# A table of offsets for the parts of a scheduled two-mixer kernel, and a larger constant for VectorE's dependent instructions

## The chip, the cores and the metric

The kernel runs on one core of a Trainium2 chip. The metric is the device time of one execution in microseconds; lower is better. Three runs of the kernel before the change give the median that is quoted, and one execution was taken by the hardware profiler.

## The reference, cut to what matters

The input x is an image batch of 4 x 256 x 64 x 64, that is 16,384 tokens of 256 channels, all in float32. Two layers follow each other; the second is a mixer and a mixture of experts.

```
# layer 0: Mamba, a selective scan over the 4,096 tokens of each image
tokens = tokens @ w_in.T
z = sigmoid(silu(tokens @ w_gate.T + b_gate))
t = layernorm(tokens)
xm, zm = split(t @ in_w.T)               # 512 + 512 channels
xm = silu(conv4(xm))                     # four taps along the tokens
dt, B, C = split(xm @ xproj_w.T)         # 16 states
h = exp(dt*A) * h + dt*x*B               # per channel and state, step by step
y = sum_n(h*C) + D*xm;  y = y * silu(zm)
x = tokens + (y @ out_w.T) * z @ w_out.T + x
# layer 1: Mamba-2 (SSD), 8 heads of 64, 64 states
xn = rmsnorm(ln(t));  z, xBC, dt = split(xn @ W_in.T);  xBC = silu(conv4(xBC))
state = state*exp(dt*A) + dt*x (x) B;  y = state.C + D*x
t = t + ln(t) + rmsnorm(y*silu(z)) @ W_out.T
# and 8 experts, top 1, capacity 2,560 tokens each, hidden 1,024
t = t + expert(ln(t)) * probability
```

## The kernel before, in words

There are three phases, one after the other: `mixers`, `experts` and `turn`. The change touches only the first.

**The mixers' work.** The tokens are cut into 64 chunks of 256, sixteen to an image. For each chunk the code records these groups of work:

- `front0`: loads the chunk (xin), makes the centred projection and the gate, the layer norm, the in-projection by m_in_w and the four-tap convolution (taps_m).
- `mid0`: stores the gates to DRAM (gx_d, z_d), makes B, C and dt (x_proj, dt_w), and stores bc_d, dt_d and u_d to DRAM. From there they come back in another layout: 32 channels times 4 states on the 128 partitions.
- `scan`: sixteen steps u = 4j + f. Each has a decay `da` (ScalarE, exp), `ub` = u4 times B (VectorE, into a PSUM tile with one buffer), for later chunks an addition of the carried state e0 to ub's first column, the scan h (VectorE, `tensor_tensor_scan`, 1,024 columns), `hlast` (ScalarE), `p` = h times C (GpSimd) and eight small products that sum p over the states into `py` (TensorE). h has three buffers, p two, da three, dt4 and u4 two, bc4 five.
- `tail0`: loads xtail and z, multiplies the gated tile g by m_out_w, and makes x1.
- `front1`: layer 1's norms (stats, logs, scale, shift), the projections by W_in, dt and the convolution (taps_x, from a copy in DRAM).
- `ssd`: layer 1's mixer in two halves s = 0 and 1 of 128 tokens: cum, decay and cdec (ScalarE and TensorE), gm, xdt and the products by decay and cdec (VectorE), the outputs and the new state.
- `back1`: out-projection, routing, and a scatter of each row to its expert's place.

Work of two chunks lies side by side: in the loop, chunk i's `front0` to `front1` are recorded beside `ssd` and `back1` of chunk i-2.

**What sets the order.** None of it is issued as it is recorded. The class `Plan` notes each instruction with an engine, a weight and its dependencies, and a list scheduler, `order()`, walks a clock of its own. When an engine is free on that clock, it takes, of the instructions whose inputs are ready and whose buffers have room, the one with the smallest key (slot, sequence number). The resulting order is the order of each engine's queue on the chip; on the chip each engine goes through its queue in that order and waits where an input is late. So the keys decide only between instructions that are ready at once, and there is no timed start. `BEHIND` is the time on that clock from the end of an instruction to a dependent one on the same engine, `SIGNAL` the same to another engine. GpSimd's p is marked `ride`: it is ordered behind the VectorE instruction before a scan, so that it runs beside the scan.

**The slots.** Sixteen slots make a chunk (`NST`). A part of the code begins with `k_.at(n)`, which sets the slot to 16i + n plus an offset found by the part's number in the chunk, `nth`, counting the calls of `at`:

```
def at(self, n):
    self.nth += 1
    r.slot(self.i * NST, n + SHIFT.get(self.nth, 0.0))
```

Counted through the code, the numbers are these. 0 to 12: front0 (0 is the load of xin, 3 and 4 the two halves of the in-projection, 6, 8, 10, 12 the convolutions). 13 and 14: the activations' call. 15 to 22: mid0 (15 is the store of gx_d and z_d, 16 x_proj, 22 the product u and its store). 23 to 26: the four bc4 loads. Then for each j from 27, 46, 65 and 84: the dt4 load, the u4 load, e0, and for each f four parts: da, ub with the scan, hlast with p, py. 103: the loads of xtail and z; 104: m_out and z; 105: x1 and stats; 106 to 121: the rest of front1 (120 is the last load of taps). 122 and 123: the second activations' call. 124 to 134: ssd (126 and 130 are cum of the two halves, 127 and 131 decay and cdec, 128 and 132 gm, xdt and their products, 129 and 133 the outputs). 135 to 141: back1 (138 and 140 are parts of the routing).

The slots that matter below are TAIL = 18 (m_out), SSD = 29, BACK = 37, FRONT0 = -25 and MID0 = -16. Before the change the table SHIFT is empty, so that every part has its plain slot. The weights on the scheduler's clock are formulas, for instance n/960 us plus 0.06 for a VectorE instruction of n columns.

**Line numbers.** Instructions of the mixers are issued by `Plan.issue`, so that the profile gives all of them line 373; they are told apart by the names of their tiles. PSUM tiles go by a (two buffers), b (one) and c (two).

Of the kernel before, what the change touches and what calls it, by code (L numbers as in the profile page):

```python
# [43 lines left out]
TAIL, SSD, BACK = 18, 29, 37  # L44
AHEAD = 4

SHIFT = {}
TOK = 4
ROW = TOK + C

# [86 lines left out]
class Plan:  # L137
# [4 lines left out]


    SIGNAL = {"DVE": 0.13, "ACT": 0.19, "PE": 0.21, "POOL": 0.12}
    BEHIND = {"DVE": 0.13, "ACT": 0.14, "PE": 0.0, "POOL": 0.13}
    LANES = 8
    SPARE = {}
    PATIENCE = 4.0
# [126 lines left out]
    def order(self):  # L275
# [34 lines left out]
        while done < len(self.ops):  # L310
# [6 lines left out]
            for e in engines:  # L317
# [40 lines left out]
                for u in op.users:  # L358
                    u.missing -= 1
                    late = op.end + (0.06 if op.lag else (self.BEHIND if u.engine == e else self.SIGNAL)[e])  # L360
                    u.ready = max(u.ready, late)
# [22 lines left out]
def tile_conv_attn_hybrid(ctx: ExitStack, tc: tile.TileContext, a: dict, out: bass.AP, cap: int, st: int):  # L384
# [45 lines left out]
    def mixers(es):  # L430
# [289 lines left out]
        class Chunk:  # L720
# [3 lines left out]
# [5 lines that stand above are left out]
# [842 lines left out]
```

## Time and profile before

| what | value |
|---|---|
| median of three runs | 6,706.08 us (6,697.39 to 6,709.94) |
| profiled execution | 6,706.9 us, span 6,704.9 us |
| mean granted TensorE clock | 0.957 |
| PE (TensorE) busy | 6,188.0 us, 92% |
| DVE (VectorE) busy | 5,552.4 us, 83% |
| ACT (ScalarE) busy | 4,879.5 us, 73% |
| POOL (GpSimd) busy | 3,295.2 us, 49% |
| first and last scan start | 80.9 us, 5,508.6 us |
| one scan, mean | 2,285 ns, 1,024 times |
| one p on GpSimd, mean | 2,355 ns, 1,024 times |
| one ub, mean | 1,250 ns, 1,024 times |

The shares are averages over the three phases, which have different limits; the mixers are read from stretches inside them. PE is the matmuls, PEld the loads of weights, which overlap them. A row of the groups gives line, engine, operation, output <- inputs, shape and count, then busy us and the mean of one in ns, then the idle time of the engine just before these instructions and what ended it. In the timeline the columns are start, length (both us), engine, line, operation and tiles, and in brackets the idle time before with what ended it.

### The profile page before, as it was taken

To read this page: it belongs to the slowest core of one execution; us is meant where nothing else is said; L and a number is where in the kernel's file an instruction comes from. 1 tells how busy PE (TensorE), PEld (TensorE's weight loads), DVE (VectorE), ACT (ScalarE), POOL (GpSimd) and SP (SyncE) were. 2 spreads that over 40 slices of the span, in tenths; PEclk is the share of its full clock that TensorE was granted. 3 is DMA by queue.
4 is the path that set the end of the run, shared out by engine and by line. 5 is a ranking of instruction groups with operands and counts; after the bars stand their busy time and mean duration, and the time that the engine had idled before them with its cause. 6 is when DMAs were issued, how large, how long until landed. Compare 5 with 4: busy or idle time off the path is not lost. (4 is left out here: it accounts for less than half of the span.)

```text
span 6704.9 us, 111610 instructions
## 1 busy us (share of the span) xinstructions
PE 6188.0 (92%) x37578; PEld 4282.6 (64%) x37578; DVE 5552.4 (83%) x7685; ACT 4879.5 (73%) x11999; POOL 3295.2 (49%) x2622
## 2 busy tenths in 40 slices
PE   7899999999999999999999999999999977999997
PEld 5566666666666666666666666666666646888886
DVE  5999999999999999999999999999999983434443
ACT  5888888888888888888888888888888863333333
POOL 4655555555555555555555555555555552333331
PEclk8999999999999999999999999999999988999998
DMA  6854445455555545455545555555555434555556
GB/s 188 234 149 150 150 147 151 146 151 152 152 153 152 149 145 151 146 150 150 152 148 150 153 153 153 153 153 152 151 153 152 149 102 143 199 199 195 200 197 260
DMA packets 924401, 1078.46 MB, mean 161 GB/s; under 512 B 93537, under 2 KB 895077, under 8 KB 912435
## 3 DMA queue, kind: packets, MB, share of 16 engines
q1 hardware_dynamic: 890002, 842.27, 42.2%
q0 software_dynamic: 29472, 212.28, 8.7%
q10 hardware_dynamic: 4352, 16.78, 0.6%
q8 instruction: 296, 4.85, 0.3%
q14 instruction: 279, 2.28, 0.1%
HBM read 787.00 MB, written 276.76 MB: 159 GB/s over the span
## 5 line engine op out<-in xcount | busy, mean ns | idle before, releaser
L373 POOL TENSOR_TENSOR p<-h,bc 128x1024 f32<-128x1024 f32 x1024 | 2411.3, 2355 | 2008.0 <-DVE ub L373 507.2
L373 DVE TENSOR_TENSOR_SCAN h<-da,ub 128x1024 f32<-128x1024 f32 x1024 | 2339.5, 2285 | 78.1 <-ACT da L373 5.8
L373 ACT ACTIVATE da<-dt,w_m_Alog 128x255 f32<-128x255 f32 x4096 | 1842.6, 503 | 0.0
L373 DVE TENSOR_TENSOR ub<-u,bc 128x1024 f32<-128x1024 f32 x1024 | 1279.7, 1250 | 13.3 <-DMA u<-u_d 5.9
L373 PE MATMUL py<-p,sum 128*32 128x256 f32 x8192 | 662.4, 396 | 183.4 <-POOL p L373 176.8
L373 PE MATMUL b<-t,w_W_in 128*128 128x256 f32 x2304 | 579.6, 392 | 25.6 <-ACT bcs L373 4.9
L373 PEld LDWEIGHTS b<-t,w_W_in 128*128 128x128 f32 x2304 | 418.7, 190 | 189.9 <-ACT raw L373 76.2
L373 PE MATMUL a<-t,w_m_in_w 128*128 128x256 f32 x2048 | 511.3, 393 | 3.1 <-DVE t L373 2.8
L1411 PE MATMUL ph<-xt,w 128*128 128x256 f32 (+1 forms) x2304 | 496.1, 368 | 12.2 <-ACT hid L1413 11.9
L373 PEld LDWEIGHTS py<-p,sum 128*32 128x32 f32 x8192 | 168.9, 108 | 508.0 <-POOL p L373 259.2
L373 PE MATMUL a<-raw,taps_m 128*128 128x256 f32 x2048 | 480.6, 382 | 4.8 <-ACT pre L373 4.8
L1422 PE MATMUL po<-w,hid 128*128 128x256 f32 x2160 | 478.0, 379 | 0.0
L373 PEld LDWEIGHTS a<-t,w_m_in_w 128*128 128x128 f32 x2048 | 371.3, 191 | 145.1 <-issue 73.3
L373 PEld LDWEIGHTS a<-raw,taps_m 128*128 128x128 f32 x2048 | 377.4, 189 | 130.1 <-ACT e L373 39.0
L1411 PEld LDWEIGHTS ph<-xt,w 128*128 128x128 f32 x2304 | 412.3, 190 | 69.5 <-ACT hid L1413 17.9
L1422 PEld LDWEIGHTS po<-w,hid 128*128 128x128 f32 x2160 | 409.7, 190 | 55.3
L373 ACT COPY hlast<-h 128x4 f32<-128x4 f32 x1024 | 202.9, 198 | 278.7 <-DVE h L373 266.1
L1385 DVE CAST number<-rows 128x2 uint32<-128x2 f32 x72 | 12.3, 170 | 450.1 <-DMA tok_d<-fixed,number 437.7
L1383 ACT ACTIVATE tn<-rows 128x256 f32<-128x256 f32 x135 | 77.4, 596 | 401.0 <-DMA rows<-buf_d,row_at 400.3
L1434 POOL DMA_INDIRECT tok_d<-fixed,number x135 | 138.5, 1026 | 402.6 <-DVE fixed L1432 265.0
L373 PE MATMUL c<-cum,after 128*128 128x512 f32 x512 | 321.1, 713 | 14.5 <-ACT dend L373 13.7
L373 ACT ACT_TABLE_LOAD x256 | 328.4, 1283 | 4.7
(237 smaller groups left out, 11312.0 us busy)
## 6 DMA issues: line engine op xcount, KB each, us to landing
dt<-dt_d SPq DMA_DIRECT2D x1024, 128.0 KB, 2.5
u<-u_d SPq DMA_DIRECT2D x1024, 128.0 KB, 2.3
raw<-raw_d SPq DMA_DIRECT2D x1024, 128.0 KB, 3.3
gx_d<-pre SPq DMA_DIRECT2D x64, 1024.0 KB, 4.5
bc<-bc_d SPq DMA_DIRECT2D x1024, 64.0 KB, 2.5
gx<-gx_d SPq DMA_DIRECT2D x256, 256.0 KB, 3.1
raw_d<-raw SPq DMA_DIRECT2D x64, 518.0 KB
dt_d<-mid SPq DMA_DIRECT2D x64, 512.0 KB, 3.2
```

Of the source, the lines that this page charges most:

```text
L373: op.issued = f(*map(placed, args), **{k: placed(v) for k, v in kw.items()})
L1383: act(tn[:, j], rows[:, j, TOK:], AF.Identity, scale=rows[:, j, 1:2], bias=rows[:, j, 2:3])
L1385: nc.vector.tensor_copy(number, rows[:, :, 3])
L1411: mm(ph, w1[:, k, f * P : (f + 1) * P], xt[:, k], start=k == 0, stop=k == KC - 1)
L1422: mm(po[:, j], hid[:, f, j * P : (j + 1) * P], w2[:, f], start=f == 0, stop=f == KF - 1)
L1434: nc.gpsimd.indirect_dma_start(out=tok_d, out_offset=bass.IndirectOffsetOnAxis(ap=number[:, j : j + 1], axis=0), in_=fixed[:, j], in_offse ...
```

## The change

Two edits. The table SHIFT, empty before, gets an offset in slots for 88 of the 142 parts, the same for each of the 64 chunks. And the scheduler's clock counts 0.17 us instead of 0.13 us from a VectorE instruction to a dependent one on VectorE. No recorded instruction, tile, buffer count or dependency differs; what differs is the order that `order()` gives to the engines' queues, and with it which instruction GpSimd's p is put behind.

```diff
-SHIFT = {}
+SHIFT = {
+    0: 3.3, 2: -0.2, 3: 1.0, 4: -0.7, 6: 0.9, 15: -2.7, 22: 0.4, 26: 5.5, 29: 0.9, 36: 0.1, 40: -0.6, 42: 0.4,
+    44: -0.1, 45: -6.6, 46: -0.1, 47: -0.1, 48: -1.1, 49: -0.4, 50: 0.2, 51: -0.1, 52: -0.1, 53: 0.9, 54: -0.1,
+    55: -0.1, 56: -0.1, 57: -0.1, 58: -0.1, 59: -0.1, 60: -0.1, 61: -1.6, 62: -0.1, 63: -0.1, 64: -0.1, 65: 0.9,
+    66: -0.1, 67: -0.1, 68: -0.1, 69: -0.1, 70: -0.1, 71: -0.4, 72: -0.1, 73: -0.1, 74: -0.1, 75: 1.2, 76: -0.1,
+    77: -0.1, 78: -0.1, 79: -0.1, 80: -2.6, 81: -0.1, 82: -0.1, 83: 3.0, 84: -0.1, 85: 1.4, 86: -0.1, 87: -0.1,
+    88: -1.9, 89: -0.1, 90: -0.1, 91: -0.1, 92: -0.1, 93: -1.1, 94: -1.7, 95: -0.5, 96: -0.1, 98: -0.1, 99: -0.1,
+    100: -0.1, 101: 0.1, 102: -0.1, 103: -7.4, 104: -2.5, 105: -0.1, 106: 0.9, 107: -0.1, 108: -0.1, 109: -0.1,
+    110: -0.1, 111: -0.1, 117: -0.1, 120: 3.4, 128: 0.9, 130: -1.4, 131: -0.6, 132: -0.1, 134: 0.3, 138: 2.0,
+    140: 0.5,
+}
...
-    BEHIND = {"DVE": 0.13, "ACT": 0.14, "PE": 0.0, "POOL": 0.13}
+    BEHIND = {"DVE": .17, "ACT": 0.14, "PE": 0.0, "POOL": 0.13}
```

## The prediction

> **What bounds the kernel now.** I read the page's table of 40 slices first: VectorE (DVE) and TensorE (PE) show a 9 in nearly every slice up to 5,500 us and the two part company only after it. So the mixers, 0 to 5,570 us, are the stage that the change can touch; the experts and the turn after it, 1,135 us, are built without the offsets. Then the busy table by stretch, whose columns are PE, PEld, DVE, ACT and POOL busy, clock and DMA:
>
> ```profile
> 1000.00:2000.00 1000.00, 937.23 (x5879) 615.91 (x5879) 926.72 (x1235) 816.13 (x2030) 521.17 (x399) 0.96 0.50 150
> 2000.00:3000.00 1000.00, 937.58 (x5951) 613.71 (x5952) 929.46 (x1226) 829.19 (x2055) 529.71 (x402) 0.96 0.51 149
> 3000.00:4000.00 1000.00, 936.12 (x5966) 612.82 (x5964) 938.04 (x1261) 830.26 (x2072) 534.20 (x414) 0.97 0.51 151
> 4000.00:5000.00 1000.00, 940.40 (x5983) 618.41 (x5981) 936.68 (x1251) 828.99 (x2068) 533.29 (x405) 0.97 0.51 152
> ```
>
> In these 4,000 us VectorE is busy 3,730.9 and TensorE 3,751.3. The groups of instructions give 750 scans, sixteen to a chunk, hence 46.9 chunks of 85.3 us. Per chunk VectorE sits idle 269.1/46.9 = **5.7 us** and TensorE 248.7/46.9 = 5.3 us. Neither is free of waits, neither has much to give: one order of work holds both. Third, VectorE's waits in the same 4,000 us (who <- for whom, us in total, times, longest):
>
> ```profile
> DVE cdec L373 <- ACT cdec L373: 62.9, 41, 3.4
> DVE stats L373 <- PE b L373: 60.5, 47, 3.9
> DVE xdt L373 <- PE c L373: 28.0, 89, 0.9
> DVE row L373 <- PE c L373: 23.2, 19, 1.3
> DVE gm L373 <- PE c L373: 14.3, 47, 0.8
> ```
>
> With the small ones this is 196.6 us, 4.2 per chunk; the other 1.5 are short gaps between VectorE's own dependent instructions. One more loss hides inside busy time:
>
> ```profile
> L373 DVE TENSOR_TENSOR decay<-decay,gm 128x1024 f32<-128x1024 f32 x93 | 178.2, 1916 | 0.0
> L373 DVE TENSOR_TENSOR decay<-decay,gm x93: 1215/1219/2833, 1017.1 to 4943.8; 128x1024 f32<-128x1024 f32 x93
> ```
>
> The mean, 1,916 ns, is far over the median of 1,219: 178.2 - 93 x 1.219 = 64.8 us, 1.4 per chunk. At most 4.2 + 1.4 + 1.5 = 7.1 us per chunk, 64 times = 454 us, could ever be won on VectorE.
>
> **What the Trainium skill says.** "SBUF — State Buffer", section "Who interferes with whom": a VectorE instruction with two SBUF inputs contends with a GpSimd instruction that reads SBUF, and the second to start blocks. The trace agrees: the decay product of 2.58 us at 4076.24 falls where GpSimd multiplies p; undisturbed ones take 1.22. "VectorE: DVE Perf Modes", section "The DRAIN you can't avoid": a semaphore between chained VectorE instructions costs nothing extra. The trace differs: in the rows near 3040 an instruction that uses its forerunner's result starts 0.13 us (ub after scan), 0.12 (e0 addition after ub) and 0.22 (scan after the addition) later than an independent one would. "Perfetto Trace Analysis", section "Tensor Engine Instruction (MATMUL, LD_WEIGHTS)": VectorE, ScalarE and GpSimd are strict FIFO. It agrees: when cdec waits 1.79 us below, the e0 addition and the scan behind it wait too.
>
> **The change part by part.** It adds and removes no instruction or byte; each item below is a move. One slot is 85.3/16 = 5.3 us, and an offset only decides between parts that are ready at once.
>
> *The constant for VectorE, 0.13 to 0.17.* The three measured spacings average 0.16, so the new number is about right. It adds at most 3 x 0.04 x 16 = 1.9 us per chunk to the order's own clock, no time on chip. It may lead the order to put a filler into some of the 1.5 us of gaps: bounds -0.5 to +0.2 us per chunk, taken **-0.15**.
>
> *Out projection two and a half slots earlier (104), second half of the SSD earlier (130: -1.4, 131: -0.6), its first half later (128: +0.9).* This is the place where the waits lie, so I read the order of time around one chunk's end:
>
> ```profile
> 4085.61 2.08 PE L373 MATMUL c<-cum,after 128*128 128x512 f32 x2
> 4087.61 1.99 PE L373 MATMUL a<-pre,w_m_xproj_w 128*64 128x256 f32 x8
> 4089.53 1.12 PE L373 MATMUL c<-cum,after 128*128 128x512 f32 x2
> 4090.59 1.08 PE L373 MATMUL c<-cum,ones 128*64 128x512 f32 x4
> 4091.60 3.72 PE L373 MATMUL b<-g,w_m_out_w 128*128 128x256 f32 x16
> ...
> 4084.33 0.68 DVE L373 TENSOR_TENSOR g<-gx,py 128x512 f32<-128x512 f32 x1
> ...
> 4092.34 0.69 DVE L373 TENSOR_TENSOR cdec<-cdec,cc 128x512 f32<-128x512 f32 x1 [1.79 <-ACT cdec L373]
> ```
>
> The gated tile g is ready at 4085.01, but its product with m_out starts 6.6 us later, behind the SSD's decays and the next chunk's x_proj. In slots, with 16i for the chunk that begins here: m_out stood at 16i+2, decays and x_proj both at 16i+1. Now m_out is at 16i-0.5, the decays at 16i+0.4, x_proj stays. m_out can start at about 4085.7, nearly 6 us sooner, and z, x1 and the layer norm's stats follow it. The stats wait, 60.5/46.9 = 1.29 us, may then go wholly or, where the order moves stats up by as much, stay: taken half, **-0.65**. The decays now stand behind m_out's 3.72 us but ahead of x_proj's 1.99: from 4085.61, 3.72 + 1.1 + 1.1 + 1.08 ends at 4092.6, where it ended at 4091.7. So the cdec wait, 1.34, is bounded by -1.3 (the order puts cdec elsewhere) and +0.9; taken **0**. Behind cdec on VectorE stand the e0 addition and the scan, and behind the scan GpSimd's p and TensorE's py. Late next is x_proj, by up to 5 us; its dt goes out to DRAM and is used most of a chunk later, which hides it. Moving gm, xdt, decay and cdec of the first half by 0.9 slots, 4.8 us, can take the decay product off GpSimd's multiply: -1.4 to +0.7 (a second product could collide), taken **-0.4**.
>
> *The routing's middle (138: +2.0, 140: +0.5).* Like 128 it moves small VectorE work behind its suppliers; the xdt, row and gm waits, 65.5/46.9 = 1.4 us, are the candidates: -1.0 to +0.5, taken **-0.3**.
>
> *Loads and stores on SP's queue (0, 15, 26, 46, 47, 65, 85, 103, 120).* At 0.4 us an issue nothing new is issued. The loads of xtail and z (-7.4) begin when their single buffers come free, in the trace 0.1 us after the last use of xtail, so they gain nothing. The last bc load (+5.5) is issued 4 u4 and dt4 groups later; it went out at 3053.77, landed about 4 us later and was first used at 3074.67: the 17 us cover it, and without them VectorE would wait one landing, 2.5 us, per chunk. xin (+3.3) has 73 us in the steady state (3009.48 to 3082.87), but in the fill it now stands behind W_in's 1,160 KB: 1.2 us of issue plus at most 6.2 us of transfer at the slice's 188 GB/s, less 2.6 us of slack: 0 to 4.8 us once, taken **+2**.
>
> *Parts of the scan (36 to 102) and of the front (2 to 6).* Most move by 0.1, which breaks ties; larger ones (45: -6.6, 83: +3.0) move the py products of one step. p has two buffers and h three, so VectorE stalls only when p falls two scans, about 10 us, behind. GpSimd's own queue (p, e0, halo copies, the scatter) keeps its contents. With 88 of 142 keys moved, some new waits must arise: 0 to +0.9 us per chunk (a fifth of what there is), taken **+0.3**.
>
> Sum per chunk: -0.15 - 0.65 + 0 - 0.4 - 0.3 + 0.3 = **-1.2 us**; 64 chunks -77, the fill +2: -75. The profiled execution took 6,706.9 us, 2.0 more than its span and 0.8 more than the median of the three runs, so one base serves for both: **6,632 us**.
>
> **The rivals.** *The wait at cdec grows (slower).* If the order leaves cdec ahead of the e0 addition, the 0.9 us computed above is paid in every chunk, and nothing is won at stats because stats moves up with x1: 64 x 0.9 = +58, **6,765 us**. For it: the calculation of 4092.6. Against: ScalarE's cum, which feeds the decays, also moves up by 1.4 slots. It decides once the decays end over 0.2 us later than now and VectorE's cdec has not moved. *TensorE is the bound.* It is as busy as VectorE, and its biggest wait is for GpSimd (py for p, 103.4 us, 2.2 per chunk), which no offset shortens; what VectorE gains TensorE's queue takes back: **6,705 us**. Against: 5.3 us of idle TensorE per chunk leave room for 1.2. *The offsets do nothing,* because buffers and data, not keys, set the starts, as for xtail and z: also 6,705. *The table removes most named waits,* 80% of 4.2 us: 64 x 3.3 = -211, **6,496 us**; against it, the order's own durations differ from the chip's, or there would be no waits now.
>
> **How the numbers follow.** A measurement of this kernel tells some 0.2%, 13 us, from no change. The forecast has 0.52, the big gain 0.08, both faster: 0.60. TensorE as the bound and offsets that do nothing have 0.10 together: no change. The growing wait has 0.30: slower. The gain's own bounds, -2.5 to -0.3 us per chunk, give 6,548 to 6,690; reaching halfway to the big gain and most of the way to the slower case, the range is 6,535 to 6,755.
>
> **What would show it right or wrong.** Right: m_out follows g by about 1 us; VectorE's busy share in the middle is near 0.945; the wait of stats is under 35 us per 4,000; decay's mean is under 1.75 us; a chunk takes 84.1 us; experts and turn keep 1,135 us. Wrong: cdec's wait over 100 us per 4,000, or a new VectorE wait for GpSimd or a DMA, or m_out still 6 us behind g.

## The result, and the profile after

The changed kernel is **slower: 6,924.93 us** median of 4 runs (6,916.91 to 6,932.59) against 6,706.42, the median of the kernel before with a fourth run of it added; the ratio is 1.0328, 95% interval 1.0310 to 1.0346. The profiled execution took 6,925.2 us, its span is 6,923.5 us.

The 218.6 us between the spans lie almost wholly inside the mixers. The first scan starts at 83.5 us (80.9 before, +2.6), the last at 5,713.6 (5,508.6), so the stretch between them grew by 202.4; after the last scan there are 1,209.9 us (1,196.3), 13.6 more, which I did not take apart. The busy table by stretch of the changed kernel (columns PE, PEld, DVE, ACT, POOL, clock, DMA):

```profile
1000.00:2000.00 1000.00, 907.70 (x5711) 601.70 (x5709) 901.46 (x1185) 801.24 (x1987) 529.70 (x390) 0.95 0.49 144
2000.00:3000.00 1000.00, 914.19 (x5714) 605.47 (x5715) 901.88 (x1184) 801.84 (x1976) 527.76 (x386) 0.94 0.49 145
3000.00:4000.00 1000.00, 913.49 (x5772) 608.39 (x5770) 902.18 (x1211) 795.13 (x1981) 527.09 (x392) 0.95 0.49 144
4000.00:5000.00 1000.00, 911.06 (x5739) 605.62 (x5738) 903.79 (x1204) 800.31 (x1995) 527.38 (x395) 0.95 0.49 146
```

TensorE and VectorE both fell, by 2.6 and 3.0 points: neither became the bound, both wait more. There are 723 scans, 45.2 chunks of **88.5 us** (85.3 before). VectorE's work per chunk is nearly the same, 79.9 us busy (79.6); its idle time grew from 5.7 to 8.6. VectorE's waits in the same 4,000 us of the changed kernel (who <- for whom, us in total, times, longest):

```profile
DVE h L383 <- POOL p L383: 102.6, 33, 3.1
DVE stats L383 <- PE b L383: 87.5, 39, 2.5
DVE pre L383 <- PE c L383: 43.2, 36, 2.0
DVE h L383 <- ACT pre L383: 28.0, 9, 3.1
DVE row L383 <- PE c L383: 18.3, 36, 0.5
DVE z L383 <- PE b L383: 13.1, 11, 2.3
...
DVE gm L383 <- PE c L383: 10.3, 14, 0.8
```

The wait for cdec, the largest before, is gone, and that for xdt too. On top stands one that the kernel before did not have: a scan waits for GpSimd's p, 33 times, 3 us each. With the nine waits of the same length that the view puts down to pre it comes 42 times in 45.2 chunks. Over the whole trace, a scan waits 0.7 us or more and starts as a p ends in 57 of the 64 chunks; it is always the fifteenth scan of the chunk, step 14, and the wait is 3.1 us on average. The timeline shows the place. First VectorE, then GpSimd, of the changed kernel (start, length, both us; in brackets the idle time and what ended it):

```profile
3037.75 2.26 DVE L383 TENSOR_TENSOR_SCAN h<-da,ub 128x1024 f32<-128x1024 f32 x1
...
3042.37 2.29 DVE L383 TENSOR_TENSOR_SCAN h<-da,ub 128x1024 f32<-128x1024 f32 x1
...
3046.34 2.29 DVE L383 TENSOR_TENSOR_SCAN h<-da,ub 128x1024 f32<-128x1024 f32 x1
...
3050.47 2.29 DVE L383 TENSOR_TENSOR_SCAN h<-da,ub 128x1024 f32<-128x1024 f32 x1
...
3058.11 2.29 DVE L383 TENSOR_TENSOR_SCAN h<-da,ub 128x1024 f32<-128x1024 f32 x1 [3.10 <-POOL p L383]
```

```profile
3042.50 2.35 POOL L383 TENSOR_TENSOR p<-h,bc 128x1024 f32<-128x1024 f32 x1 [0.72 <-DMA raw<-raw_d]
...
3050.24 1.07 POOL L272 DMA_INDIRECT buf_d<-row,dest  x1 [2.21 <-DVE dest L383]
3051.34 2.37 POOL L383 TENSOR_TENSOR p<-h,bc 128x1024 f32<-128x1024 f32 x1
3053.88 1.81 POOL L272 DMA_INDIRECT buf_d<-row,dest  x1 [0.17 <-issue]
3055.72 2.36 POOL L383 TENSOR_TENSOR p<-h,bc 128x1024 f32<-128x1024 f32 x1
```

The five scans are those of steps 10, **12, 11**, 13 and 14: entry 88 (-1.9) moves step 12's ub and scan from slot 12 to 10.1, ahead of step 11's at 10.9. Parts 89 and 90, the p and py of step 12, got -0.1 only, so the p's keep the order 10, **11, 12**. Step 12's h is made from 3042.37 to 3044.66 and read by the last p above, 3055.72 to 3058.08, with two scatters (1.07 and 1.81 us) and step 11's p ahead of it in GpSimd's queue; before the first scatter GpSimd stood idle for 2.21 us, until VectorE had made dest. Scan 14 starts 0.03 us after that p's end. Its ub was ready and VectorE free from 3055.01; what it waited for was a buffer.

When scan 14 is due, h's three buffers hold the steps 12, 11 and 13, and step 11's p had ended at 3053.71, 1.3 us before the wait began: one buffer **was** free. The scheduler counts only how many are free, and by that count it may well place scan 14 there. Which buffer a tile gets is decided later, by the tile pool as the instructions are issued, and the pool had given scan 14 that of step 12, the scan three places earlier in the new order. Read from the addresses in the built program, this is so in 59 of the 64 chunks; the trace has the wait in 57. By which rule the pool picks a buffer was not examined.

### The profile page after: what moved, and what is told of

Read it like the earlier page. It is cut to its first block, busy times and chain, and to the rows that moved or that the text cites. A ratio compares the mean times of both kernels' runs of the same rounds, so it can differ in the third digit from the quotient of the medians.

```text
span 6923.5 us, 111359 instructions
## 1 busy us (share of the span) xinstructions
PE 6247.6 (90%) x37578; PEld 4361.9 (63%) x37578; DVE 5572.9 (80%) x7685; ACT 4894.7 (71%) x11999; POOL 3378.6 (49%) x2622
## 3 DMA queue, kind: packets, MB, share of 16 engines
q1 hardware_dynamic: 890002, 842.27, 41.2%
## 5 line engine op out<-in xcount | busy, mean ns | idle before, releaser
L383 ACT ACTIVATE da<-dt,w_m_Alog 128x255 f32<-128x255 f32 x4096 | 1815.3, 502 | 0.5 <-DMA bc<-bc_d 0.2
L383 DVE TENSOR_TENSOR ub<-u,bc 128x1024 f32<-128x1024 f32 x1024 | 1294.2, 1264 | 15.6 <-DMA u<-u_d 7.7
L383 PE MATMUL py<-p,sum 128*32 128x256 f32 x8192 | 689.7, 417 | 185.3 <-POOL p L383 184.7
L383 PE MATMUL a<-raw,taps_m 128*128 128x256 f32 x2048 | 569.4, 433 | 4.9 <-ACT pre L383 4.9
L383 PEld LDWEIGHTS a<-raw,taps_m 128*128 128x128 f32 x2048 | 429.7, 216 | 138.9 <-issue 55.9
L383 PE MATMUL a<-t,w_m_in_w 128*128 128x256 f32 x2048 | 496.7, 391 | 3.1 <-DVE t L383 2.8
L1395 DVE CAST number<-rows 128x2 uint32<-128x2 f32 x72 | 12.3, 170 | 456.0 <-DMA tok_d<-fixed,number 443.8
L383 PE MATMUL c<-cum,after 128*128 128x512 f32 x512 | 289.8, 651 | 66.2 <-ACT dend L383 62.5
```

What stands on the lines that cost most here:

```text
L383: op.issued = f(*map(placed, args), **{k: placed(v) for k, v in kw.items()})
L1395: nc.vector.tensor_copy(number, rows[:, :, 3])
```

## The experiments

Times are medians; ratios are to runs of the kernel before on the same chip, with 95% intervals. "Waits" are VectorE's, per 4,000 us in the middle.

### Which part costs: the constant, entry 88, the rest of the table

The theories were A, the swap of scans; B, the constant; C, many small moves.

e1: the kernel before with the constant 0.17 and no table.

> The kernel before with the clock constant alone (0.17, table empty). Theory A (the swap: the offset of part 88 takes scan 12 ahead of scan 11, while their products p keep the old order, so that h's buffer of scan 12 is held too long): the constant has no part in it; 6,650 to 6,760 us, and VectorE's scan waits for GpSimd's p under 10 us per 4,000. Theory B (the constant spoils the order by counting VectorE longer): at least half of the 218 us of the whole change, so 6,815 or more. Theory C (many small moves on TensorE and ScalarE): like A here, near 6,706.

Measured 6,711.54 us, 1.0022 (1.0014 to 1.0030): the constant alone is too small for B.

e2: the whole table with the constant 0.13.

> The table alone, with the constant at 0.13. Theory A: the swap is there, so most of the loss is: 6,850 to 6,950 us, with the wait of scan for p at 70 us or more per 4,000. Theory B: under 6,800. Theory C: 6,850 to 6,950 as in A, but with the wait for p not the largest.

Measured 6,712.39, 1.0015 (1.0005 to 1.0026): the table alone costs next to nothing, and the wait for p is not among VectorE's waits. Neither A nor C allowed this, and B, which did, fails by e1. Each half of the change costs 0.2%, both together 3.3%.

e3: the change without entry 88.

```diff
-    88: -1.9, 89: -0.1, 90: -0.1,
+    89: -0.1, 90: -0.1,
```

> The changed kernel without the one entry of part 88 (ub and scan of step 12, -1.9), so that the scans stand in the order of their numbers again. Theory A: the waits of scan for p (102.6) and for ScalarE's pre (28.0), together 2.9 us per chunk, go to under 15 us per 4,000, which is worth 64 x 2.9 = 185 us: 6,740 us, 6,700 to 6,790. Theory B and theory C: one entry of 88 is worth little, 6,870 to 6,930.

Measured **6,636.80, 0.9915 (0.9897 to 0.9934)**: one entry of the 88 turns a gain of 0.85% into a loss of 3.3%. This version beats both kernels, and by more than A expected (6,700 to 6,790). It has no wait for p; its largest waits are cdec 42.8 us, row 29.8 and stats 28.6.

e4: the kernel before with `SHIFT = {88: -1.9}`.

> The kernel before with the one entry 88: -1.9 and nothing else. Theory A: the swap alone brings the wait of scan for p, 60 to 130 us per 4,000, that is 1.3 to 2.9 us per chunk, and 6,790 to 6,890 us. Theories B and C: 6,680 to 6,740, one entry being worth little.

Measured 6,725.13, 1.0043 (1.0029 to 1.0057). The swap alone costs only 0.4%, which A did not allow. Its wait for p comes 3 times in the 4,000 us.

Two more cells complete the eight. e7: the table without 88, constant 0.13. e8: entry 88 and the constant 0.17, nothing else.

> The table without part 88, and the constant at 0.13: does the gain that the table without part 88 shows at 0.17 (6,637 us against 6,697) need the constant? Theory F (the gain is the table's): 6,620 to 6,670. Rival G (table and constant only fit together): 6,690 to 6,760.

> The kernel before with the constant at 0.17 and the one entry 88: -1.9. The swap with 0.13 cost 28 us (6,725 against 6,697), the constant alone 14. Theory D, if the constant is what makes p of step 12 late enough for scan 14 to wait: wait of scan for p over 50 us per 4,000 and 6,770 to 6,880 us. Rival H (it takes other entries of the table too, which crowd GpSimd's queue there): wait under 30 us per 4,000 and 6,710 to 6,760.

Measured 6,849.93, 1.0216 (1.0199 to 1.0233), and 6,841.63, 1.0215 (1.0198 to 1.0233). Neither F nor G allowed the first; in the second the wait for p is 61.8 us, as D expected. All eight, with the number of chunks in which scan 14 was given step 12's buffer (from the built programs). The traces agree: they have the wait of scan 14 for a p in 7 and 29 chunks of the second row, in 1 and 57 of the last, and in none of the cells with 0.

| rest of table | entry 88 | constant 0.13 | constant 0.17 |
|---|---|---|---|
| no | no | 1 (0) | 1.0022 (0) |
| no | yes | 1.0043 (7) | 1.0215 (29) |
| yes | no | 1.0216 (0) | 0.9915 (0) |
| yes | yes | 1.0015 (6) | 1.0328 (59) |

Entry 88 gains 2% in one cell and costs 4% in the next. Along the column 0.17 the loss follows the count; in the column 0.13 it does not: e7 loses 2.2% with no such buffer. Its ub products take 21.4 us per chunk instead of 19.9 (but 21.2 in e1, which loses 0.2%), its largest waits are stats 50.2 us, gm 41.2 and t 30.9, and its granted clock is as low as the changed kernel's, 0.942 and 0.943 in the profiled executions. The cause of that loss was not tested further. Nor was it examined why the same crossing gets step 12's buffer in 6 chunks with one constant and in 59 with the other.

### Is it the buffers, or the swap of the scans?

Theory D: the scheduler's count and the pool's hand-out differ, and that is the loss. Theory E: the swap itself, or the rest of the table.

e5: the p and py of step 12 follow their scan, so that both orders are swapped alike.

```diff
-    88: -1.9, 89: -0.1, 90: -0.1,
+    88: -1.9, 89: -1.9, 90: -1.9,
```

> The changed kernel with parts 89 and 90 (p and py of step 12) moved by -1.9 like part 88, so that p of step 12 stands ahead of p of step 11, as the scans do. Theory D (rotation: the scheduler counts how many of h's three buffers are free, the pool hands them out in turn; with scans 12, 11 and products 11, 12 scan 14 gets the buffer of step 12, whose p is the later one, and waits though step 11's is free): the wait of scan for p falls from 102.6 to under 15 us per 4,000, and the time to 6,640 to 6,760 us. Rival E (the swap of the scans itself, or the rest of the table, costs the time on TensorE and ScalarE, the wait for p only shows it): 6,860 to 6,930, with other waits in its place.

Measured 6,657.72, 0.9932 (0.9915 to 0.9948), no wait for p: the early scan is not bad in itself. But e5 has another order of all queues, so it doesn't isolate the buffers. e6 does: every queue as in the changed kernel, and only which of three h tiles a step gets is different, the one whose p comes first. In the two traces the sequence of operations and tile names on VectorE, ScalarE and GpSimd is the same from end to end, and on TensorE too, where a run of equal matmuls is counted as one.

```diff
-                    h = work([P, SQ, T], "h", 3)
+                    h = h_tile(k_.i * NST + u)
...
+        def h_tile(n):
+            def make():
+                k = next(h_turn)
+                h_of[n] = k if k < 3 else h_of[k - 3]
+                return h_bufs[h_of[n]]
```

> The changed kernel with every queue in the same order, but h's three buffers given to the scans in the order in which the products p free them, not in turn: scan 14 takes the buffer of step 11. Theory D: wait of scan for p under 15 us per 4,000, 6,640 to 6,760 us. Rival E: since no instruction has moved, 6,860 to 6,930, with the idle time of VectorE gone to other waits.

Measured 6,773.22, 1.0103 (1.0086 to 1.0119): **152 us less than the changed kernel**, 13 us over the range that D gave and far from E's. VectorE's waits in e6:

```profile
DVE stats L383 <- PE b L383: 106.3, 40, 4.1
DVE gm L383 <- PE c L383: 26.2, 31, 1.5
DVE z L383 <- PE b L383: 21.1, 23, 2.3
```

The wait for p is gone from the list, and the scans' whole idle time falls from 170.5 to 47.6 us. The reverse, e11: e2's queues unchanged (by the traces too), and the h tiles given strictly in turn, so that step 14 always gets step 12's.

```diff
-                    h = work([P, SQ, T], "h", 3)
+                    h = h_tile()          # h_bufs[next(h_turn) % 3]
```

> The table with the constant at 0.13 (6,712 us), every queue in the same order, but h's three buffers given strictly in turn. In the built programs the pool gave scan 14 the buffer of step 12, whose p is the later one, in 59 of 64 chunks of the changed kernel, in 6 of this one, in 29 of the constant with part 88. Theory D: with the buffer of step 12 in all 64 chunks the wait of scan for p appears, 60 to 130 us per 4,000, and 6,800 to 6,900 us. Rival E (the buffer only shows a lateness that is there anyway): 6,700 to 6,740.

Measured 6,778.66, 1.0133 (1.0106 to 1.0160), 66 us more than e2, less than expected. Its waits:

```profile
DVE h L383 <- POOL p L383: 104.4, 44, 2.6
DVE stats L383 <- PE b L383: 44.4, 43, 2.4
```

The wait comes back, once a chunk. So D is shown both ways with the queues held fixed. The idle time at the scans rises by 2.10 us per chunk, 134 us in 64 chunks, yet the kernel loses 66: stats' wait shrinks by 1.15 and row's by 0.57 us per chunk. Stats' supplier does not come sooner because it had more time. In both kernels the sixteen matmuls of x1, which stats reads, begin 12.2 or 12.3 us behind the end of g, but they last 4.0 us in e11 and 5.1 in e2, at a mean granted clock of 0.95 and 0.75 in that stretch. What row's wait owes was not examined.

### The prediction's largest step, part 104

e9: the kernel before with `SHIFT = {104: -2.5}`. Theory I: waits move along rather than vanish.

> The kernel before with 104: -2.5 alone (m_out and z earlier). The prediction's step: the stats wait falls by half, 0.65 us per chunk, cdec's wait stays within 0 to +0.9: 6,700 - 42 = 6,660 us, at most 6,640 to 6,760. Theory I (the waits at stats are where the order believes x1 to be ready too early, and move with it): stats wait as before, 60 us per 4,000 or more, and 6,690 to 6,740.

Measured **6,840.32, 1.0208 (1.0172 to 1.0243)**: my largest gain alone is a loss of 143 us, outside both ranges. VectorE's waits in e9, then one chunk's TensorE, then VectorE:

```profile
DVE stats L375 <- PE b L375: 150.5, 46, 4.0
DVE gm L375 <- PE c L375: 53.1, 46, 1.4
DVE z L375 <- PE b L375: 27.1, 33, 1.0
```

```profile
3046.03 4.37 PE L375 MATMUL b<-g,w_m_out_w 128*128 128x256 f32 x16
3050.23 1.02 PE L375 MATMUL c<-cum,after 128*128 128x512 f32 x2
...
3052.09 1.89 PE L375 MATMUL a<-pre,w_m_xproj_w 128*64 128x256 f32 x8
...
3058.67 2.08 PE L375 MATMUL b<-w_w_in,xtail 128*128 128x256 f32 x4
...
3063.95 1.36 PE L375 MATMUL b<-w_w_out,z 128*128 128x256 f32 x4
```

```profile
3055.01 0.29 DVE L375 TENSOR_TENSOR gm<-c,upto 128x128 f32<-128x128 f32 x1 [1.39 <-PE c L375]
...
3065.34 0.76 DVE L375 BATCH_NORM_STATS2 stats<-b 128x6 f32<-128x256 f32 x2 [3.98 <-PE b L375]
```

m_out is early, right after g, as the key says. Decays, x_proj and gm's supplier then stand behind its 4.4 us, and gm waits. x1 (part 105), whose key did not move, is still made from 3058.67 to 3065.31, in four pieces, while VectorE's order has stats right behind the scan that ended at 3061.37. The wait for cdec (62.9 before) is zero; stats' grew by 90.0.

But x1 is also slow here. Below are the busy table's row (its last columns are clock, DMA share and GB/s) and half of x1's matmuls, first of this stretch of e9, then of the same stretch in the chunk of the kernel before that the prediction reads:

```profile
3058.60:3065.40 6.80, 6.80 (x21) 5.20 (x24) 2.69 (x4) 5.65 (x12) 2.75 (x3) 0.56 0.36 111
L375 PE MATMUL b<-w_w_in,xtail x8: 634/634/795, 3058.7 to 3063.5; 128*128 128x256 f32 x8
```

```profile
4098.90:4102.70 3.80, 3.80 (x21) 3.07 (x24) 3.45 (x4) 3.80 (x9) 2.38 (x2) 1.00 0.44 122
L373 PE MATMUL b<-w_w_in,xtail x8: 379/379/483, 4098.9 to 4101.4; 128*128 128x256 f32 x8
```

At a granted clock of 0.56 a matmul of x1 has a median of 634 ns, at 1.00 of 379. Over all whole chunks of the 4,000 us, x1 starts 14.3 us behind the end of g (13.6 in the kernel before) and lasts 5.8 us (4.7), and VectorE is free for stats at 16.8 us (17.1). So of the 2.0 us per chunk that stats' wait grew by, about 0.6 are x1's later start, 1.1 its slower matmuls and 0.3 VectorE's coming earlier. The kernel before shows the same: where x1 has a mean clock under 0.75 (28 chunks) stats waits 2.0 us on average, in the other 19 chunks 0.2. What brings the clock down in this stretch was not tested.

e10: the three SSD entries 128, 130 and 131 alone. e12: the 49 entries of -0.1 alone (theory J: they shift waits without changing the sum; K: they are what matters).

> The kernel before with 128: 0.9, 130: -1.4 and 131: -0.6 alone. The prediction's steps: cdec's wait unchanged, decay 0.4 us per chunk cheaper, 6,675 us. From the changed kernel, where cdec's wait all but went (1.34 to 0.04 us per chunk): 1.3 us less per chunk, 6,617 us. Theory I (waits move elsewhere): 6,680 to 6,730.

> The kernel before with the 49 entries of -0.1 alone, which can do no more than break ties. The prediction took the many small moves as +0.3 us per chunk of new waits: 6,719 us. Theory J (any other order of this kernel lies within 1% either way, by which waits it happens to draw): 6,640 to 6,770 with the single waits of VectorE changed by 20 us per 4,000 and more. Theory K (ties do nothing): 6,690 to 6,710 and the waits as before.

For e10 measured 6,657.59, 0.9936 (0.9917 to 0.9955), a gain of 40 us between the two forecasts, with cdec's wait down from 62.9 to 24.2; for e12 6,702.84, 1.0010 (1.0000 to 1.0021), with single waits changed (stats 1.29 to 0.43 us per chunk, pre 0 to 1.14) and the time hardly: J.

Whether 104 also explains what e6 still loses, 73 us, was asked of three kernels that lack only that entry: e13 from e6, e14 from e3, e15 from the changed kernel. Theory L: it costs in every order. Theory M: single entries don't add up.

> After with the h buffers taken in the order in which the p's free them and without the offset of part 104; it has an order of its own. Theory L (the out projection's move is what the by-free version still loses): alone it cost 143 us, so without it the 73 us over the kernel before go, 6,600 to 6,710. Theory M (single entries don't add up; the 73 us belong to the whole order): over 6,750, as with it. The wait of stats tells: L under 1.5 us per chunk (2.3 with the entry), M 2 or more.

> After without the entries 88 and 104. Theory L: the entry costs in every order, so that this beats the version without 88 alone (6,637): 6,500 to 6,610. Theory M: what 104 costs alone says nothing of what it costs here: 6,600 to 6,800, and if over 6,680 the entry that lost 143 us alone is a gain in company.

> After without entry 104 alone; 88 stays, and with it the pool's own handing out of h. Theory D (handed-out buffers): if scan 14 gets the buffer of step 12 in most chunks, the wait for p stays, 60 us or more per 4,000, and the time is 6,750 to 6,930. Theory L adds a fall of 100 us or more from 6,925. Theory M: no lower than 6,880.

| kernel | with 104 | without 104 | entry 104 is worth |
|---|---|---|---|
| before | 6,840.32 | 6,697.21 | +143 us |
| changed | 6,924.93 | 6,840.58, 1.0197 (1.0173 to 1.0222) | +84 us |
| changed, h by its p's (e6) | 6,773.22 | 6,730.14, 1.0046 (1.0030 to 1.0063) | +43 us |
| changed without 88 (e3) | 6,636.80 | 6,733.62, 1.0055 (1.0038 to 1.0072) | **-97 us** |

L fails: three losses and one gain, the gain in the best order found. M's ranges hold for e14 alone. In e13 the stats wait falls from 2.30 to 0.33 us per chunk, as L said (x1's mean clock is 0.97 there and 0.73 in e6), but pre (0.12 to 1.36) and cdec (0.04 to 1.09) grow by 2.3 between them. e15, where step 14 gets step 12's buffer in 58 chunks, keeps the wait of D:

```profile
DVE h L383 <- POOL p L383: 124.3, 40, 3.1
DVE pre L383 <- PE c L383: 75.7, 56, 3.6
DVE cdec L383 <- ACT cdec L383: 41.4, 43, 2.0
```

So 152 us of the loss are the handed-out buffers (e6). Of the 73 us by which e6 stays above its own runs of the kernel before (6,700.44), 43 go with 104 (e13); the last 29, and what in the order makes an entry gain or lose, stay open. The granted clock is a candidate that no run here isolates (the next section comes back to it).

## Why the prediction was wrong

The forecast of 6,632 us fails by 293 us, and the range ends at 6,755. Step by step, in us per chunk of VectorE:

| step | predicted | changed kernel |
|---|---|---|
| constant | -0.15 | no price of its own: +14 us alone, -213 us from e7 to e3, +213 us from e2 to the change |
| stats (m_out earlier) | -0.65 | +0.65 |
| cdec | 0 (-1.3 to +0.9) | -1.30 |
| decay product | -0.4 (-1.4 to +0.7) | +0.21 |
| xdt, row and gm | -0.3 (-1.0 to +0.5) | -0.37, all idle time before the three |
| new waits | +0.3 (0 to +0.9) | h +2.65, pre +0.96, z +0.25: **+3.9** |

**The step that failed is "Parts of the scan"**, and in it the sentence "p has two buffers and h three, so VectorE stalls only when p falls two scans, about 10 us, behind". It did not single out entry 88, though -1.9 is more than the 1.1 slots to the scan before it (12 to 10.9), while its p stays. The margin was counted in buffers, as the scheduler counts them, not by which buffer a scan gets: with the crossing what counts is the distance from step 12's scan to its own p, 13.4 us from start to start, and the pool hands out that one. The bound of +0.9 was "a fifth of what there is", a share of the old waits; one new wait of 3 us in every chunk does not scale with those. The list of what would make the forecast wrong did name "a new VectorE wait for GpSimd", but no rival priced it.

**The second is the sign of part 104.** The calculation that m_out could start about 1 us after g was right; here g ends at 3077.19:

```profile
3079.02 3.62 PE L383 MATMUL b<-g,w_m_out_w 128*128 128x256 f32 x16
3082.48 1.02 PE L383 MATMUL c<-cum,after 128*128 128x512 f32 x2
```

The start fell from 6.6 us behind g to 1.8 in these two chunks, and from 5.7 to 1.3 on average. "z, x1 and the layer norm's stats follow it" was right for z, which is done 3.8 us sooner behind g, but hardly for x1, whose own offset is -0.1: it starts 1.3 us sooner (12.3 us behind g instead of 13.6) and lasts 5.0 us instead of 4.7, while VectorE is free for stats 1.5 us sooner. And what the 3.7 to 4.4 us of m_out push back, gm's supplier among it, was priced at cdec alone. The worst end that I allowed for stats was "the order moves stats up by as much", no gain; that stats moves up further than its supplier was not considered, nor that x1's matmuls take longer where the granted clock is low; there stats waited before the change, too (e9).

**Right, or inside its bounds:** the fill (+2 us; the first scan starts 2.6 later), cdec's bound of -1.3 (reached), the waits of xdt, row and gm, and the lower chance for the cdec rival: its wait vanished. The decay product missed the value taken and stayed inside the bounds; its group and its spread in the changed kernel:

```profile
L383 DVE TENSOR_TENSOR decay<-decay,gm 128x1024 f32<-128x1024 f32 x90 | 181.5, 2017 | 0.0
L383 DVE TENSOR_TENSOR decay<-decay,gm x90: 1211/1219/3068, 1023.2 to 4944.6; 128x1024 f32<-128x1024 f32 x90
```

The median is untouched, the mean 101 ns longer: the excess, 181.5 - 90 x 1.219 = 71.8 us or 1.6 per chunk, is about what it was (1.4), so the move of 0.9 slots took the product off no multiply. The Trainium skill's "Perfetto Trace Analysis", section "Tensor Engine Instruction (MATMUL, LD_WEIGHTS)", has VectorE, ScalarE and GpSimd as strict FIFO. The wait of scan 14 agrees and gives it a price: the p that held the buffer had its h from 3044.66 on and started 11.1 us later, behind other work in GpSimd's queue and through 2.21 us in which GpSimd was idle.

**No term for the granted clock.** It fell from 0.957 to 0.943. The median of a matmul does not show it, for the clock is low in stretches (0.56 in the one of e9 above): of the matmuls of a 128x256 tile with 128*128 weights, whose median is 379 ns, 3.0% took over 500 ns in the middle 4,000 us of the kernel before and 8.5% in the changed one, 6.9% in e9, 9.4% in e7 and 1.9% in e3. TensorE's busy time per chunk went from 80.0 to 80.7 us. Whether an order loses because its matmuls meet a low clock, or the clock is low because of the waits in that order, no run here tells. For the handed-out buffers it is no rival: e11 has no lower clock than e2 (0.962 and 0.958 in the profiled executions), and the wait for p came all the same.

## What to carry to other kernels

Where a scheduler counts free buffers and a pool hands them out later, any key that lets a producer overtake another, while their consumers keep their order, can make the count wrong: move the consumers' keys with it (e5, whose order differs in other places too), or take the buffer whose reader comes first (e6). Offsets found together have no prices one by one: the same entry was worth +143 and -97 us in two orders, so a table is tested whole, again for each constant of the scheduler, and with its entries taken out from the full version. An earlier product is no gain by itself: ask whether the last supplier of its consumers comes with it, what now stands behind it in the same queue, and how fast that supplier's matmuls run there; the mean clock of the whole execution does not tell.

## What the runs showed that I had not expected

The prediction had a decay product of 2.58 us beside a p. A product of half its size, 128x512, which takes 0.68 us elsewhere, took 2.60 us where two of GpSimd's p's ran in a row. VectorE and GpSimd of the changed kernel:

```profile
3065.63 2.60 DVE L383 TENSOR_TENSOR cdec<-cdec,cc 128x512 f32<-128x512 f32 x1
```

```profile
3063.02 4.66 POOL L383 TENSOR_TENSOR p<-h,bc 128x1024 f32<-128x1024 f32 x2 [4.94 <-DVE ub L383]
```

It ended at 3068.23, 0.55 us after the second p (3067.68). This agrees with the Trainium skill's "SBUF — State Buffer", section "Who interferes with whom", which has the second of two such instructions block.

And the issue of a scatter is not a fixed cost on GpSimd: its mean is 1,065 ns in the kernel before and 1,473 ns in the changed one, with 1.81 us for the second in the timeline above, which lay in the queue ahead of the p that scan 14 waited for. What lengthens it was not tested.
